# First context's loads pinned among the second projections, and six banks for the first four accumulators

## The chip, the cores and the metric

The kernel runs on one core of a Trainium2 chip. The metric is the time of one execution on the device in microseconds (us). Before the change it is 2506.7 us, the median of three runs (2506.53 to 2509.44).

Engine names as in the profile: PE is TensorE (PEld its weight loads), DVE is VectorE, ACT is ScalarE, POOL is GpSimd, SP is SyncE, which issues nearly all transfers here. Each engine and each queue takes its instructions in order.

## The reference

A decoder layer on x (8 sequences of 100 tokens, width 1024) in three blocks, each followed by "add and layer norm". Cut to what matters here:

```
x1 = layernorm(x + attn(x))              # retention, 8 heads
q, k, v = x1 @ wq, x1 @ wk, x1 @ wv      # "second projections": 16 q heads, 4 k and v heads of 128
q, k = rope(rms_norm(q)), rope(rms_norm(k))
k_ctx, v_ctx = rms_norm(ctx @ wk_ctx), ctx @ wv_ctx     # ctx: 722 rows per sequence
o = softmax(q @ [k_ctx, k].T * scale + causal mask) @ [v_ctx, v]
x2 = layernorm(x1 + o @ wo)
out = layernorm(x2 + (silu(x2 @ w_gate.T) * (x2 @ w_up.T)) @ w_down.T)
```

## The kernel before

Activations lie with their features on the 128 partitions. The 800 tokens are two halves of N = 400 (four sequences each). To keep the precision of float32, every operand is split in a high part (a rounded copy, made by ScalarE, line 67) and a low part (the difference, made by VectorE, line 68), and each product takes three matmuls (`mm3`, lines 86 to 88). A projection of one 128-wide block of outputs for one half (`proj`, lines 100 to 105) is thus 8 x 3 = 24 matmuls into one accumulator bank. PSUM has eight banks, given out by tag: three of "a", four of "s", one of "v" (line 50).

**The place of the change** is the passage from the first block to the second. `out_proj` (lines 217 to 251) computes the output projection of the first attention and the norm after it, half by half. For half 1 the norm is split into parts (`norm_early`, `norm_more`, `norm_late`): seven of the eight blocks of y are centred early (line 298), the last is added at line 240, the correction of the mean comes as a matmul (line 306), those of the variance at lines 300 and 307. Then follow the subtraction of that correction (line 317), the root (`inv_root`, lines 110 to 122: Ln, Exp, Square on ScalarE, lines 113, 116 and 118, and two steps on VectorE, lines 119 and 121), eight multiplications (line 272), eight splits into the tiles z1[1], and eight stores to zd (line 275).

**The second projections** (lines 624 to 655) run over the four key heads kv. Each has six weights w2[kv, i] (i = 0 to 3 queries, 4 keys, 5 values), loaded in groups, for kv = 0 as 0 to 3 and then 4 and 5. Within a group the two halves follow each other, and each half runs over the group's i. One pass of the innermost loop is called a *unit* here; kv = 0 has twelve. A unit is a projection, and then its drain:

- ScalarE squares the accumulator (line 646); GpSimd sums the squares over the partitions (`all_red`, line 126, tile ss).
- `rope` (lines 129 to 139): ScalarE copies the accumulator with its halves swapped into t2 (lines 134 and 135); VectorE multiplies the accumulator by the cosines into t1 (line 136), t2 by the sines (137), and adds the two (138).
- `inv_root` gives the factor r; VectorE multiplies (line 651); the result is split into d, and SP stores it (line 655).
- The unit i = 5 is transposed instead, split and stored (lines 640 to 643).

The accumulator's bank is free once lines 646, 134, 135 and 136 have read it. In this kernel every unit takes its accumulator from the three banks "a"; t2 and r are both PSUM banks with tag "s" (`swapped=` and `at=`).

**The context.** `load_context(b)` brings the context of sequence b: two halves hf of four transfers (tile cs, of the tag "wst" with three buffers, which the weight loads use too), each split into tiles of the tag "big". For sequence 0 it is called ahead of the units i = 4 and 5 of kv = 0 (line 628). Its first reader is `context_keys` in kv = 1 (lines 630 to 634; hf 0 first), the second is in kv = 2.

**The order.** The code is traced in this order, and a planner then sets the order on each engine with simulated times (line 1091), so that instructions move ahead of work written before them. `tc.keep_in_program_order(i)` takes that freedom from i in one direction: i stays behind the instruction that was traced last on the same engine before it. Where the planner finds work for TensorE and where a transfer is issued thus depend on what it believes to be ready.

Of the kernel before, what the change touches and what calls it, by code (L numbers as in the profile page):

```python
# [19 lines left out]
N = NB * T  # L20
KT = D // P
QT = KT // 2
SC, SH = 722, 362
# [16 lines left out]
def decoder_layer(ctx, tc, xT, cT, w1, wo1, w2, wo2, wc, w3, wd, gw, qw, kw, trig, dec, mask, out):  # L40
    nc = tc.nc

    def sbuf(name, bufs, side=None):
        return tc.tile_pool(name=name, bufs=bufs, side=side, reuse_waits="tile")
# [8 lines left out]
    def bank(tag):  # L53
        return ps.tile([P, 512], F32, tag=tag, name=tag, bufs=banks[tag])

    def f32(ap):
        return ap.bitcast(F32)

    def bt(ap):
        return ap.rearrange("p (b t) -> p b t", b=NB)  # L60

    def split(dst, src):

        split2(dst[:, 0], dst[:, 1], src)
# [5 lines left out]
    def load_w(src, w=None, parts=1):  # L70
        st = wp.tile([P, KT * P], F32, tag="wst", name="wst", bufs=3)
        if w is None:
            w = wp.tile([P, 2, KT * P], FR, tag="w", name="w", bufs=4)
        for i in range(parts):
            c = slice(i * KT * P // parts, (i + 1) * KT * P // parts)
            nc.sync.dma_start(out=st[:, c], in_=src[:, c])
            split(w[:, :, c], st[:, c])
        return w
# [11 lines left out]
    def mmw(acc, w, k, rh, rl, start, stop):  # L90
        c = slice(k * P, (k + 1) * P)
        mm3(acc, w[:, 0, c], w[:, 1, c], rh, rl, start, stop)
# [3 lines left out]
    def acc_tag():  # L96
        turn[0] += 1
        return "as"[turn[0] % 2]

    def proj(w, z, n=N, tag="a"):  # L100
        acc = bank(tag)[:, :n]
        for k in range(KT):
            t = z[k // QT]
            mmw(acc, w, k, t[:, 0, k % QT, :n], t[:, 1, k % QT, :n], k == 0, k == KT - 1)
        return acc
# [4 lines left out]
    def inv_root(pool, ss, eps, n=N, pin=False, at=None):  # L110

        r = pool.tile([P, n], F32, tag="r0", name="r0") if at is None else at
        ln = nc.scalar.activation(r, ss, AF.Ln, bias=eps)
        if pin:
            tc.keep_in_program_order(ln)
        nc.scalar.activation(r, r, AF.Exp, scale=-0.5)
        q = pool.tile([P, n], F32, tag="r1", name="r1")
        nc.scalar.activation(q, r, AF.Square)
        nc.vector.scalar_tensor_tensor(q, ss, eps, q, ALU.add, ALU.mult)
        out = q if at is None else at  # L120
        nc.vector.scalar_tensor_tensor(out, q, 3.0, r, ALU.subtract, ALU.mult)
        return out
# [6 lines left out]
    def rope(pool, acc, cosw, sinw, tag="t1", op=ALU.add, swapped=None):  # L129

        t1 = pool.tile([P, N], F32, tag=tag, name=tag)
        t2 = pool.tile([P, N], F32, tag="t2", name="t2") if swapped is None else swapped
        h = P // 2
        nc.scalar.copy(t2[0:h], acc[h:P])
        nc.scalar.copy(t2[h:P], acc[0:h])
        nc.vector.tensor_tensor(bt(t1), bt(acc), cosw[:, None, :].to_broadcast([P, NB, T]), ALU.mult)  # L136
        nc.vector.tensor_tensor(bt(t2), bt(t2), sinw[:, None, :].to_broadcast([P, NB, T]), ALU.mult)
        nc.vector.tensor_tensor(t1, t1, t2, op)
        return t1
# [26 lines left out]
    def big(shape):  # L166
        return bp.tile(shape, FR, tag="big", name="big")
# [9 lines left out]
    def const(v, name):  # L177
        t = cp.tile([P, 1], F32, name=name)
        nc.vector.memset(t, v)
        return t  # L180
# [3 lines left out]
    eps_k = const(128e-6, "eps_k")  # L184
# [238 lines left out]
    with sbuf("l1", 2) as p:  # L423
# [42 lines left out]
        qk, v, oo, ss = {}, {}, {}, {}  # L466
# [104 lines left out]
    with sbuf("ln1", 1) as p:  # L571
        z1 = [out_proj(half, wo1, load_o1, xT, p, 2, p, lambda _: [z1p.tile([P, 2, QT, N], FR, tag="z", name="z")
                                                                 for _ in range(2)], zd) for half in range(2)]
# [3 lines left out]
    ka = kapool.__enter__()  # L577
    cz = []

    def load_context(b):  # L580

        cz.clear()
        for hf in range(2):
            n = SN[hf]
            z = [big([P, 2, QT, SH]) for _ in range(2)]
            for k in range(0, KT, 2):
                cs = wp.tile([P, KT * P], F32, tag="wst", name="cs", bufs=3)
                cs = cs[:, :2 * n].rearrange("p (k n) -> p k n", k=2)
                nc.sync.dma_start(out=cs, in_=cT[b, :, k:k + 2, hf * SH:hf * SH + n])
                split(z[k // QT][:, :, k % QT:k % QT + 2, :n], cs)  # L590
            cz.append(z)

    def context_keys(kv):

        kall = ka.tile([P, 2, SC + T], FR, tag="kall", name="kall")
        wk = load_ws(2 * kv)
        sq = ka.tile([P, SC], F32, tag="ksq", name="ksq", bufs=1)
        ss = ka.tile([P, 6 * P], F32, tag="kss", name="kss", bufs=1)
        row = dr.tile([6, P], F32, tag="row", name="row", bufs=2)
        nc.gpsimd.memset(ss[:, SC:], 1.0)  # L600

        def step(hf):
            n, at = SN[hf], slice(hf * SH, hf * SH + SN[hf])
            acc = proj(wk, cz[hf], n)
            nc.scalar.activation(sq[:, at], acc, AF.Square)  # L605
            nc.gpsimd.partition_all_reduce(ss[:, at], sq[:, at], P, RED.add)  # L606
            nc.scalar.activation(kall[:, 0, at], acc, AF.Copy, scale=kws)
            nc.vector.scalar_tensor_tensor(kall[:, 1, at], acc, kws, f32(kall[:, 0, at]), ALU.mult, ALU.subtract)
            if hf:
                nc.sync.dma_start(out=row.rearrange("c p -> (c p)")[None, :], in_=ss[0:1])  # L610
        return step, (kall, row)
# [9 lines left out]


    early = []
    with sbuf("l2", 2) as p:
        for kv in range(NKV):
            for i0, i1 in ((0, 4), (4, 6)) if kv == 0 else ((0, 2), (2, 4), (4, 6)):
                if (kv, i0) == (0, 4):
                    load_context(0)
                ws = [load_w(w2[kv, i]) for i in range(i0, i1)]
                if (kv, i0) in ((1, 2), (2, 2)):  # L630
                    step, kept = context_keys(kv - 1)
                    early.append(kept)
                if (kv, i0) in ((1, 2), (2, 0), (2, 2), (3, 0)):
                    step(i0 == 0)
                for half in range(2):
                    bs = slice(half * NB, (half + 1) * NB)
                    for i in range(i0, i1):
                        acc = proj(ws[i - i0], z1[half])
                        if i == 5:
                            tr = tokens_first(p, acc).rearrange("p (b d) -> p b d", b=NB)  # L640
                            vs = p.tile([T, NB, 2, P], FR, tag="vs", name="vs", bufs=1)
                            split2(vs[:, :, 0], vs[:, :, 1], tr)
                            nc.sync.dma_start(out=f32(vd[kv, :, bs]), in_=f32(vs))
                            continue
                        sq = p.tile([P, N], F32, tag="sq", name="sq")
                        nc.scalar.activation(sq, acc, AF.Square)
                        ss = all_red(p, sq, "ss")
                        tb = tq if i < 4 else tk
                        t = rope(p, acc, tb[:, 0], tb[:, 1], swapped=bank("s")[:, :N])
                        r = inv_root(p, ss, eps_k, at=bank("s")[:, :N])  # L650
                        nc.vector.scalar_tensor_tensor(
                            t, t, -0.5 if i < 4 else -0.5 * math.sqrt(P), r, ALU.mult, ALU.mult)
                        d = p.tile([P, NB, 2, T], FR, tag="d", name="d", bufs=3)
                        split2(d[:, :, 0], d[:, :, 1], bt(t))
                        nc.sync.dma_start(out=f32(qd[kv, i, :, bs] if i < 4 else kd[kv, :, bs]), in_=f32(d))
# [5 lines left out]
    with sbuf("cx", 2) as p, sbuf("c1", 1) as p1:  # L661
# [6 lines left out]
        for b in range(B):  # L668
            if b > 0:
                load_context(b)  # L670
            for kv in range(NKV):
                if early:
                    kall, row = early.pop(0)
                else:
# [9 lines left out]
                                  in_=f32(qd[kv, :, :, b]).rearrange("h p l t -> p h (l t)"))  # L684
# [21 lines left out]
                s = p1.tile([P, NC, N], F32, tag="s", name="s")  # L706
# [5 lines left out]
                for j, c in enumerate(ORDER):  # L712
                    rows, n, t0 = (R6, N6, T6) if c == 6 else (P, N, 0)
# [35 lines left out]
                for j in (1, 0, 2, 3, 4, 5, 6):  # L749
                    c = ORDER[j]  # L750
                    n = N6 if c == 6 else N
# [4 lines left out]
                r = p.tile([P, N], F32, bufs=1, tag="r0", name="r0")  # L756
# [72 lines left out]
    ws = [[load_w(w3[i, part]) for part in range(2)] for i in range(2)]  # L829
    gs = {}  # L830
    for half in range(2):
        for i in range(2):
            ag, au = (proj(w, z2[half], tag=acc_tag()) for w in ws[i])
            t = temp()
# [163 lines left out]
    with sbuf("ln3", 2, "right") as lnp:  # L998
        ws = []
        for half in range(2):  # L1000
# [3 lines left out]
            for m in range(KT):  # L1004
# [7 lines left out]
                acc = proj(ws[m], z3[half], tag=acc_tag())  # L1012
# [83 lines left out]
```

## Time and profile before

| What | Value |
|---|---|
| median of three runs | 2506.7 us |
| the profiled execution's own time | 2508.7 us |
| its span, first to last instruction | 2506.9 us |
| instructions | 37175 |
| mean granted TensorE clock | 0.995 of full speed |
| all eight cs loads of the first context: casts, subtractions | 64 of each in the whole kernel, 8 between 583.6 and 606.3 us |
| second projections, units of kv = 0 | 575.9 to about 663 us |
| L67 cast of a cs tile, mean | 794 ns on ACT |
| L68 subtraction of a cs tile | 902 to 915 ns on DVE |
| L126 all-reduce of ss, median | 2604 ns on POOL |

The page cuts the span into 40 slices of 63 us, a digit for each: the busy share in tenths (9 is 90% or more).

```profile
PE   8999999997999999999999999999999999999997
DVE  7677877567877688989999999866987777666756
POOL 0111111001445343433434434100000000000000
DMA  7333445774543654554554563675455444389731
```

The tenth slice, 564 to 627 us, holds the passage described above. It is the only one between the first and the last in which TensorE's digit is 7.

### The profile page before, as it was taken

What the parts mean: (1) busy time and instruction counts of PE and PEld (TensorE: products, weight loads), DVE (VectorE), ACT (ScalarE), POOL (GpSimd) and SP (SyncE); (2) the same over time, 40 slices, a digit from 0 to 9 for tenths busy, and PEclk for the clock granted to TensorE, in tenths of its full rate; (3) what the DMA queues carried; (4) which work ended last, traced back from release to release, by engine and by line L of the source; (5) the groups of instructions that cost most, each with busy time, mean ns of one, the idle gap of its engine ahead of it and who ended that gap; (6) DMA issues with size and microseconds to landing.
All of it is one profiled execution on the core that took longest, in us unless ns stands there. A gap on an engine that the chain in (4) does not pass through costs nothing.

```text
span 2506.9 us, 37175 instructions
## 1 busy us (share of the span) xinstructions
PE 2456.2 (98%) x14036; PEld 2435.6 (97%) x14036; DVE 1952.7 (78%) x3110; ACT 1342.0 (54%) x2264; POOL 464.8 (19%) x234
## 2 busy tenths in 40 slices
PE   8999999997999999999999999999999999999997
PEld 8999999997999999999999999999999999999997
DVE  7677877567877688989999999866987777666756
ACT  6667676334767556656566666533544445432221
POOL 0111111001445343433434434100000000000000
PEclk9999999998999999999999999999999999999999
DMA  7333445774543654554554563675455444389731
GB/s 241 111 111 128 134 142 184 241 271 128 170 148 131 215 175 152 166 171 146 165 185 133 174 196 119 208 254 162 136 179 193 168 168 163 120 293 331 261 101 53
DMA packets 224450, 433.96 MB, mean 173 GB/s; under 512 B 47338, under 2 KB 168042, under 8 KB 211854
## 3 DMA queue, kind: packets, MB, share of 16 engines
q1 hardware_dynamic: 223118, 427.39, 51.0%
q0 software_dynamic: 1152, 4.19, 1.1%
q8 instruction: 110, 1.80, 0.3%
q14 instruction: 70, 0.57, 0.1%
HBM read 322.18 MB, written 109.35 MB: 172 GB/s over the span
## 4 chain that ended last, share of the span: by engine, by line
PE 92%; DVE 3%; DMA 2%; ACT 1%; issue 1%; POOL 0%; SPq 0%; DVEq 0%; POOLq 0%
PE a L88 19%; PE a L86 19%; PE a L87 19%; PE s L88 9%; PE s L87 9%; PE s L86 9%; PE v L88 2%; PE v L86 2%; PE v L87 2%; PE s L492 1%; PE s L689 1%; PE s L149 1%; DVE w L68 1%; DMA tp<-in_xT 0%; PE v L484 0%
## 5 line engine op out<-in xcount | busy, mean ns | idle before, releaser
L86 PE MATMUL a<-big,w 128*128 128x400 f32 (+2 forms) x1808 | 610.3, 338 | 10.9 <-ACT big L67 6.8
L87 PE MATMUL a<-big,w 128*128 128x400 f32 (+2 forms) x1808 | 610.2, 338 | 0.0
L88 PE MATMUL a<-big,w 128*128 128x400 f32 (+2 forms) x1808 | 608.5, 337 | 0.0
L67 ACT CAST w<-wst 128x1024 fp32r<-128x1024 f32 (+1 forms) x231 | 239.6, 1039 | 392.9 <-PE a L88 148.7
L68 DVE TENSOR_TENSOR w<-wst,w 128x1024 fp32r<-128x1024 f32 (+1 forms) x231 | 282.7, 1225 | 135.7 <-ACT w L67 134.7
L86 PEld LDWEIGHTS a<-big,w 128*128 128x128 f32 x1808 | 340.5, 188 | 12.9 <-ACT big L67 6.8
L87 PEld LDWEIGHTS a<-big,w 128*128 128x128 f32 x1808 | 341.1, 189 | 1.5 <-DVE big L68 0.6
L88 PEld LDWEIGHTS a<-big,w 128*128 128x128 f32 x1808 | 341.0, 189 | 0.6
L86 PE MATMUL a<-z,w 128*128 128x400 f32 x680 | 235.0, 346 | 21.1 <-DVE t L136 18.6
L88 PE MATMUL a<-z,w 128*128 128x400 f32 x680 | 235.9, 347 | 0.0
L87 PE MATMUL a<-z,w 128*128 128x400 f32 x680 | 235.8, 347 | 0.0
L86 PE MATMUL s<-big,w 128*128 128x400 f32 x664 | 230.5, 347 | 0.1
L88 PE MATMUL s<-big,w 128*128 128x400 f32 x664 | 229.0, 346 | 0.4 <-DVE w L68 0.4
L87 PE MATMUL s<-big,w 128*128 128x400 f32 x664 | 229.1, 345 | 0.0
L126 POOL PARTITION_ALL_REDUCE ss<-sq x56 | 151.2, 2702 | 332.3 <-DMA zd<-y 171.0
L606 POOL PARTITION_ALL_REDUCE kss<-ksq x64 | 166.3, 2599 | 128.6 <-ACT ksq L605 128.1
L86 PEld LDWEIGHTS a<-z,w 128*128 128x128 f32 x680 | 128.3, 189 | 22.9 <-DVE t L136 15.9
L723 ACT ACTIVATE s<-s,rk 128x400 f32<-128x400 f32 x160 | 87.9, 591 | 94.9 <-DVE sm L743 68.6
L88 PEld LDWEIGHTS a<-z,w 128*128 128x128 f32 x680 | 129.0, 190 | 0.3
L87 PEld LDWEIGHTS a<-z,w 128*128 128x128 f32 x680 | 128.3, 189 | 0.2
L86 PEld LDWEIGHTS s<-big,w 128*128 128x128 f32 x664 | 124.6, 188 | 1.4 <-ACT w L67 0.4
L88 PEld LDWEIGHTS s<-big,w 128*128 128x128 f32 x664 | 125.1, 188 | 0.7 <-DVE w L68 0.7
(331 smaller groups left out, 5427.0 us busy)
## 6 DMA issues: line engine op xcount, KB each, us to landing
wst<-in_w SPq DMA_DIRECT2D x135, 512.0 KB
w<-wcd SPq DMA_DIRECT2D x64, 1024.0 KB
wst<-in_wo SPq DMA_DIRECT2D x64, 512.0 KB
hd<-h SPq DMA_DIRECT2D x12, 1400.0 KB
wst<-in_wd SPq DMA_DIRECT2D x64, 256.0 KB
big<-o1d SPq DMA_DIRECT2D x16, 800.0 KB
qd<-d SPq DMA_DIRECT2D x32, 400.0 KB
q<-qd SPq DMA_DIRECT2D x32, 400.0 KB
```

Source lines behind the costliest of these rows:

```text
L67: nc.scalar.copy(hi, src)
L68: nc.vector.tensor_tensor(lo, src, f32(hi), ALU.subtract)
L86: nc.tensor.matmul(acc, lh, rh, start=start, stop=False, skip_group_check=chain)
L87: nc.tensor.matmul(acc, lh, rl, start=False, stop=False, skip_group_check=chain)
L88: nc.tensor.matmul(acc, ll, rh, start=False, stop=stop, skip_group_check=chain)
L126: nc.gpsimd.partition_all_reduce(y, x, P, op)
L149: nc.tensor.transpose(tr[0:T, b * P:(b + 1) * P], vt[:, b * T:(b + 1) * T], ident)
L492: nc.tensor.matmul(bt(o)[:, b], vv[:, b * P:(b + 1) * P], pf[:, b], start=True, stop=True)
L606: nc.gpsimd.partition_all_reduce(ss[:, at], sq[:, at], P, RED.add)
L689: nc.tensor.transpose(tr[0:rows, (c - c0) * P:(c - c0 + 1) * P], vt[:, c * P:c * P + rows], ident)
L723: nc.scalar.activation(sc, sp, AF.Copy, scale=rk[:, c:c + 1])
```

## The change

Three things. `load_context` becomes a generator, `context_steps`, which stops after each transfer and its split; other sequences still run it through at once. For sequence 0 a step is taken ahead of each of eight units of kv = 0 (the four of half 1 in the first group, then the four of i = 4 and 5), and its transfer is kept in program order on SP's queue. The four units of the first group's half 0 (`first`) take their accumulators in turn from the tags "s" and "a" (`acc_tag`), and have t2 and r in SBUF tiles of the pool l2 (the tags "t2" and "r0", which were not used there) in place of two PSUM banks.

```diff
-    def load_context(b):
+    def context_steps(b, pinned=False):
 
         cz.clear()
         for hf in range(2):
...
             for k in range(0, KT, 2):
                 cs = wp.tile([P, KT * P], F32, tag="wst", name="cs", bufs=3)
                 cs = cs[:, :2 * n].rearrange("p (k n) -> p k n", k=2)
-                nc.sync.dma_start(out=cs, in_=cT[b, :, k:k + 2, hf * SH:hf * SH + n])
+                i = nc.sync.dma_start(out=cs, in_=cT[b, :, k:k + 2, hf * SH:hf * SH + n])
+                if pinned:
+                    tc.keep_in_program_order(i)
                 split(z[k // QT][:, :, k % QT:k % QT + 2, :n], cs)
-            cz.append(z)
+                if k == 0:
+                    cz.append(z)
+                yield
+
+    def load_context(b):
+        for _ in context_steps(b):
+            pass
...
     early = []
+    ctx0 = context_steps(0, True)
     with sbuf("l2", 2) as p:
         for kv in range(NKV):
             for i0, i1 in ((0, 4), (4, 6)) if kv == 0 else ((0, 2), (2, 4), (4, 6)):
-                if (kv, i0) == (0, 4):
-                    load_context(0)
                 ws = [load_w(w2[kv, i]) for i in range(i0, i1)]
...
                 for half in range(2):
                     bs = slice(half * NB, (half + 1) * NB)
+
+                    first = (kv, i0, half) == (0, 0, 0)
                     for i in range(i0, i1):
-                        acc = proj(ws[i - i0], z1[half])
+                        if kv == 0 and (half == 1 or i0 == 4):
+                            next(ctx0, None)
+                        acc = proj(ws[i - i0], z1[half], tag=acc_tag() if first else "a")
...
-                        t = rope(p, acc, tb[:, 0], tb[:, 1], swapped=bank("s")[:, :N])
-                        r = inv_root(p, ss, eps_k, at=bank("s")[:, :N])
+                        t = rope(p, acc, tb[:, 0], tb[:, 1], swapped=None if first else bank("s")[:, :N])
+                        r = inv_root(p, ss, eps_k, at=None if first else bank("s")[:, :N])
```

## The prediction

> **What bounds the kernel.** Page first: the engines' busy times. Then the waits of TensorE, which say where its idle time lies; then the stretch in question by windows; then the chain that ended last, in order of time; last the timelines of VectorE and GpSimd.
>
> ```profile
> PE 2456.2 (98%) x14036; PEld 2435.6 (97%) x14036; DVE 1952.7 (78%) x3110; ACT 1342.0 (54%) x2264; POOL 464.8 (19%) x234
> ...
> PE a L86 <- DVE t L136: 18.6, 3, 15.6
> ```
>
> TensorE is busy for 2456.2 of 2506.9 us. Of the 50.7 us of idle time, one wait has 15.6: a matmul into an accumulator bank ("a") that VectorE's L136 must first have read. The windows (columns: length, then busy us of PE, PE's weight load, DVE, ACT, POOL, then the granted clock) put it at the passage from the first norm to the second projections:
>
> ```profile
> 600.00:606.40 6.40, 0.48 (x3) 0.15 (x1) 4.46 (x7) 3.19 (x5) 0.00 (x0) 0.78 0.58 187
> 606.40:615.50 9.10, 0.00 (x0) 0.00 (x0) 9.01 (x19) 5.76 (x12) 2.77 (x1) 0.50 0.74 262
> 615.50:630.00 14.50, 12.53 (x56) 12.19 (x57) 10.94 (x20) 10.26 (x22) 10.32 (x4) 0.82 0.07 28
> 630.00:660.00 30.00, 27.01 (x150) 26.35 (x148) 28.33 (x48) 23.58 (x45) 14.47 (x6) 1.00 0.49 167
> 660.00:690.00 30.00, 29.46 (x166) 29.10 (x165) 23.86 (x40) 20.86 (x41) 14.55 (x6) 1.00 0.53 174
> ```
>
> PE loses 5.92 + 9.10 + 1.97 + 2.99 + 0.54 = 20.5 us between 600 and 690. It also runs 13 matmuls after the long wait at 0.333 us apart (616.10 to 620.6) where they take 0.182 later: 2.0 us. So **22.5 us** is all that this place can give. From 630 to 660 VectorE is busy for 28.33 of 30 us: there, the drain of the units bounds, not TensorE. From 660 on it is not (23.86 of 30).
>
> Why does the drain begin only at 615.5? The chain (start, length, what):
>
> ```profile
> 585.87 0.84 DVE big L68
> 586.72 3.30 DMA cs<-in_cT
> 590.04 0.81 ACT big L67
> 590.88 0.93 DVE big L68
> 591.82 3.18 DMA cs<-in_cT
> 595.02 0.81 ACT big L67
> 595.85 0.91 DVE big L68
> 596.76 1.22 DVE y L317 x3
> ...
> 600.53 0.91 DVE big L68
> 601.46 3.11 DMA cs<-in_cT
> 604.59 0.79 ACT big L67
> ```
>
> These are the eight loads of the first context ("cs") and their splits. They are written after the first eight units, but the planner has put them in the middle of the norm of half 1. Their three buffers go round in a ring (load, cast, subtract, load), and VectorE and ScalarE, whose queues go in order, stand behind them. The norm's Ln is at 603.59, its factor is ready at 607.7, z1[1] is complete at 615.5, and only then does VectorE run the first L136.
>
> **The change, part by part.** Call the twelve units of kv = 0 u0 to u11 in program order; each is 24 matmuls, 4.4 us. From the rows, PE started u3 at 616.1, u4 at 622.6, u5 at 628.5, u8 at 643.0, u9 at 649.5, u10 at 653.9.
>
> *Loads out of the norm.* VectorE loses eight subtractions (7.09 us busy up to 606.4), ScalarE eight casts (6.36 us). What is late next: the last block of the output projection, whose accumulator is added at 590.12 (L240, 0.57). From there the norm's own steps: square 0.54, variance matmul 0.83, L314 0.57, Ln, Exp, Square 0.63 + 0.53 + 0.54, L119 and L121 0.64 + 0.57, eight L272 3.97, eight subtractions of z 3.97; the eight L317 (3.93) fit beside ScalarE's part but for about 0.5. Sum: 590.69 + 13.3 = 604.0 instead of 615.5, 11.5 us earlier. Against that: in the trace the mean's correction (L306) was ready at 590.7 and stood in PE's queue until 594.11. If that 3.4 us stays, the gain is 8. I take 10.2, somewhat above the middle, since the planner times that matmul by VectorE's work, which shrinks. Ends: 8 and 11.5.
>
> *Six banks.* u0 to u3 take s, a, s, a instead of a only; with the third "a", u4 needs no drained bank either. u3 runs at 600.1 instead of 616.1, and u4 follows at 604.5 if z1[1] is there (its first slices are ready soon after the last L272, and then come every 0.5 us, PE takes one each 0.55). So the 15.6 us hole closes as such. But u5 needs u1's L136, u6 u3's, and from u7 on the pairing is the old one (u8 after u5, u9 after u6). Shift the old L136 times (u1 620.6, u3 630.4, u4 635.5, u5 642.3, u6 648.8) by 10.2: u5 starts at 611 (2 us of idle time), u6 at 621 (about 5), u8 at 633, u9 at 639, u10 at 644. TensorE is ahead, then waits again for VectorE: the unit of matmuls that was brought forward is worth nothing in itself. **What counts is the shift of the drain**, because u9 <- u6 is the last wait that binds.
>
> *The loads in their new place.* Each cs load stands on SP's queue behind the last SP instruction traced before it: the first four behind the store of d of u3 to u6, the fifth behind the weight load of i = 5, the last three behind the stores of u8, u9, u10. Old d subtractions end at 639.7 for u3, 647.9 for u4; less 10.2 and plus 3.2 to land (chain above), cs 0 is split at 633, cs 1 at 641. Ahead of u6's L136 (638.6) lie cs 0 and cs 4: 2 x 0.91 = 1.8 us of VectorE. The rest falls where VectorE has 6 us in 30 free, and u10 had some 2 us to spare (u7's L136 at 651.2 for a start at 653.9). First use of the context is the projection whose square is at 686.0, of its second half later; both have tens of us. SP: the weight loads behind a cs wait for nothing new, as each d store was in that queue before.
>
> *t2 and r0 in SBUF for u0 to u3.* Durations alike: L137 takes 574 ns with PSUM, 569 ns where both tiles were in SBUF. But here a rule speaks against the change. The trace first:
>
> ```profile
> 625.24 2.60 POOL L126 PARTITION_ALL_REDUCE ss<-sq  x1 [0.35 <-ACT sq L646]
> ...
> 625.26 2.15 DVE L68 TENSOR_TENSOR d<-t,d 128x400 fp32r<-128x400 f32 x1
> ...
> 640.14 2.28 DVE L68 TENSOR_TENSOR w<-wst,w 128x1024 fp32r<-128x1024 f32 x1
> ```
>
> The subtraction of d takes 0.57 elsewhere; begun with an all-reduce it took 2.15. The one of w, 1.22 elsewhere, took 2.28. The Trainium skill ("SBUF — State Buffer", Who interferes with whom) says that a VectorE instruction with two SBUF inputs shares a read interface with a GpSimd instruction that reads SBUF, and that the second to start is blocked until the first is finished. With t2 and r in PSUM, L137, L138, L121 and L651 had one SBUF input; now 16 instructions have two. By the rule each of four all-reduces could hold VectorE for its 2.6 us: 10.4. The trace is milder: the one above was held 1.6, and the subtraction of w at 632.34, 1.7 us into an all-reduce begun at 630.66, took its normal 1.22. So at most 1.6 for each reduce, 6.4 in all; new hits only where an instruction falls in its first part. I take one, 1.2 us (1.1 and 1.6 were seen); ends 0 and 6.4.
>
> *Rest.* The generator and cz cost nothing on the chip. The four extra tiles may lie where y lay: at most 2.4 us (a store's landing in the chain), once, before u0's L136, and hidden behind z's subtractions; taken as 0.
>
> **Sum**: -10.2 + 1.8 + 1.2 = **-7.2 us**; the profiled span 2506.9 becomes 2499.7, its own time 2508.7 becomes 2501.5, and from the median 2506.7 it is **2499.5**. A change below 0.2% (5.0 us) can't be told from none here. With all ends favourable: -11.5 - 2.7 (stretched subtractions that miss the reduces) = -14; unfavourable: -8 + 1.8 + 6.4 = 0.
>
> **Rivals.** *R1, no change (0.23):* the drain gives it back. All eight splits end up ahead of u6 or u9 in VectorE's order (7.2 us), or the reduces hold several of the new instructions. 10.2 - 7.2 - 3 = 0: 2506.7. For it: VectorE 28.33 of 30; against: the queue order above.
>
> *R2, slower (0.17):* the planner believes a cs load lands sooner than it does. Its cast then stands at the head of ScalarE's queue, the subtraction at that of VectorE's, and the drains behind both wait. Before, ScalarE waited 5.2 us for these eight loads (0.65 each, 1.7 at most), with the loads issued early; now each is issued late, one at a time, and a full landing is 3.2. It decides from 7.2 + 2 (spare) over 8 = 1.2 us each; at 2.2 it costs 17.6 - 9.2 = +8: 2515. Against: the planner now has other work to put in front.
>
> *R3, much faster (0.12):* the planner, with four accumulators in hand, orders the drains so that VectorE has no holes (it idled 3.46 us before u1's L136), and PE stays fed: some 16 of the 22.5 us: 2490.5.
>
> **Numbers.** Forecast 0.48 at 2499.5 (its own range 2493 to 2504). Faster by over 0.2%: most of it (0.45) and R3, 0.57. Within: the rest of it, R1 without its slow tail: 0.25. Slower: 0.18. Range 2490 to 2510: below lies half of R3, above most of R2.
>
> **What would show it.** Right: no cs rows before 606; z's subtractions ending near 605; u3 at once after u2; PE waits for L136 of 2 to 5 us each around 610 to 640, and no wait over 8; VectorE full until some 650; the clock dips less than 0.50. Wrong: ScalarE waiting for cs between 625 and 665 (R2); all-reduces beside L137, L138, L121 or L651 of 1.5 us and more (R1); or the norm no earlier, because PE's queue holds L306 and L300.

## The result

The changed kernel takes 2538.85 us (median of four runs, 2537.49 to 2539.44), the one before 2506.68 beside it: a ratio of 1.0125, with a 95% interval from 1.0113 to 1.0138. It is 32 us slower; the forecast was 7 us faster. The profiled execution took 2537.49 us, with a span of 2535.7.

From the page of the changed kernel, the busy times and two rows of slices:

```profile
PE 2459.5 (97%) x14036; PEld 2437.7 (96%) x14036; DVE 1961.2 (77%) x3110; ACT 1343.7 (53%) x2264; POOL 465.8 (18%) x234
...
PE   8999999998499999999999999999999999999997
...
PEclk9999999999799999999999999999999999999999
```

Little has become longer as work: TensorE is busy for 3.3 us more, of which the sum below puts 1.8 down to its slower clock after waits; the rest is not accounted for. The new idle time lies in one slice, the eleventh (634 to 697 us), which has gone from 9 to 4, and the passage from the norm that was at 7 is now at 8. The waits of TensorE (us in total, times, longest):

```profile
PE a L86 <- ACT w L67: 35.7, 6, 19.7
PE a L86 <- DVE t L136: 10.7, 2, 10.4
```

The wait for a bank (L136, 18.6 before) has shrunk. A wait for *weights* (ScalarE's cast of w, 1.8 us in all before) has grown to 35.7. The windows of the changed kernel (length, then busy us of PE, PE's weight load, DVE, ACT, POOL, then the granted clock) show when:

```profile
600.00:610.00 10.00, 9.69 (x54) 9.36 (x53) 9.96 (x18) 7.03 (x15) 6.85 (x2) 1.00 0.41 149
610.00:620.00 10.00, 3.79 (x21) 3.46 (x19) 9.79 (x14) 7.70 (x16) 6.66 (x3) 0.84 0.11 41
620.00:630.00 10.00, 5.84 (x25) 5.84 (x26) 10.00 (x15) 6.30 (x13) 5.71 (x2) 0.65 0.21 82
630.00:640.00 10.00, 4.43 (x25) 4.10 (x23) 8.91 (x15) 6.59 (x14) 4.68 (x2) 0.86 0.59 187
640.00:650.00 10.00, 0.00 (x0) 0.00 (x0) 7.34 (x13) 4.67 (x9) 0.89 (x1) 0.50 0.42 116
650.00:660.00 10.00, 5.68 (x22) 5.13 (x23) 4.28 (x4) 3.68 (x4) 0.00 (x0) 0.62 0.57 195
...
680.00:690.00 10.00, 0.51 (x2) 0.50 (x2) 2.54 (x5) 2.71 (x4) 0.00 (x0) 0.50 0.73 226
```

The first row is what the change aims at: TensorE works through 600 to 610, where it stood before. Then come three holes. In the first, VectorE is full (9.79 of 10, 10.00): a drain is late. In the second, VectorE and ScalarE run dry too (from 8.91 and 6.59 down to 4.28 and 3.68), and in the third they do little (2.54 and 2.71): no compute engine is full there. The chain of the changed kernel through these two (start, length, what):

```profile
646.83 0.32 SPq L666
647.24 0.39 SPq L589
647.72 5.26 DMA wst<-in_w
653.00 1.05 ACT w L67
654.07 1.24 DVE w L68
655.35 0.70 PE a L88
...
681.73 0.34 SPq L666
682.12 0.43 SPq L589
682.59 5.78 DMA wst<-in_w
688.40 1.05 ACT w L67
689.48 1.24 DVE w L68
690.75 0.70 PE a L88
```

Twice the same six steps: a store of d (L666), a pinned load of the context (L589), and only then the load of weights, with its landing, cast and subtraction, on which TensorE waits. SyncE's own timeline of the changed kernel shows the queue:

```profile
646.83 0.32 SPq L666 DMA_DIRECT2D qd<-d  x1
647.24 0.39 SPq L589 DMA_DIRECT2D cs<-in_cT  x1
647.72 1.08 SPq L76 DMA_DIRECT2D wst<-in_w  x2
...
682.12 0.43 SPq L589 DMA_DIRECT2D cs<-in_cT  x1
682.59 15.64 SPq L76 DMA_DIRECT2D wst<-in_w  x7
```

The two weights of i = 4 and 5 are issued after cs 3 (the load at 647.24), and seven more weight loads, those of kv = 1 first, in a row after cs 7 (682.12). Before, the context's loads were through by 602, and three weight loads went out right behind them, some 40 us ahead of the first unit with i = 4 (643.05):

```profile
578.39 23.44 SPq L589 DMA_DIRECT2D cs<-in_cT  x8
602.28 4.40 SPq L76 DMA_DIRECT2D wst<-in_w  x3
```

In the changed kernel the loads stand in the order in which the buffers of the tag "wst" were asked for in the code: cs 0 to 3, two weights, cs 4 to 7, further weights. It is the place in the queue that costs, more than an occupied buffer. If the three buffers go round in that order, the first of the two weights takes that of cs 1, whose subtraction ended at 641.39. By this estimate its load could have gone out 6.3 us earlier than 647.72, had it not stood behind cs 3 and the store ahead of cs 3.

The sum: TensorE's waits between 600 and 715 are 46.0 us (0.3 + 10.4 + 19.7 + 0.2 + 1.4 + 13.2 + 0.2 + 0.6) against 20.5 before, 25.5 more. Twenty-four matmuls follow waits at half rate (3.6 us lost) against twelve (1.8). Together 27.3 of the 28.8 us between the two spans (2535.7 and 2506.9).

### The profile page after: what moved, and what is told of

Read it like the earlier page. It is cut to its first block, busy times and chain, and to the rows that moved or that the text cites. A ratio compares the mean times of both kernels' runs of the same rounds, so it can differ in the third digit from the quotient of the medians.

```text
span 2535.7 us, 37151 instructions
## 1 busy us (share of the span) xinstructions
PE 2459.5 (97%) x14036; PEld 2437.7 (96%) x14036; DVE 1961.2 (77%) x3110; ACT 1343.7 (53%) x2264; POOL 465.8 (18%) x234
## 4 chain that ended last, share of the span: by engine, by line
PE 92%; DVE 4%; DMA 2%; ACT 1%; issue 1%; SPq 0%; DVEq 0%; ACTq 0%
PE a L88 19%; PE a L86 19%; PE a L87 19%; PE s L88 9%; PE s L87 9%; PE s L86 9%; PE v L88 2%; PE v L86 2%; PE v L87 2%; PE s L492 1%; PE s L700 1%; DMA wst<-in_w 1%; PE s L149 1%; DMA tp<-in_xT 0%; PE v L484 0%
## 5 line engine op out<-in xcount | busy, mean ns | idle before, releaser
L86 PE MATMUL a<-z,w 128*128 128x400 f32 x664 | 230.8, 348 | 45.8 <-ACT w L67 35.1
L88 PE MATMUL a<-z,w 128*128 128x400 f32 x664 | 231.4, 349 | 0.5 <-DVE w L68 0.5
L87 PE MATMUL a<-z,w 128*128 128x400 f32 x664 | 231.3, 348 | 0.0
L86 PEld LDWEIGHTS a<-z,w 128*128 128x128 f32 x664 | 126.3, 190 | 47.7 <-ACT w L67 36.4
L88 PEld LDWEIGHTS a<-z,w 128*128 128x128 f32 x664 | 126.9, 191 | 1.6 <-DVE w L68 1.5
L87 PEld LDWEIGHTS a<-z,w 128*128 128x128 f32 x664 | 126.2, 190 | 0.0
```

Of the source, the lines that this page charges most:

```text
L86: nc.tensor.matmul(acc, lh, rh, start=start, stop=False, skip_group_check=chain)
L87: nc.tensor.matmul(acc, lh, rl, start=False, stop=False, skip_group_check=chain)
L88: nc.tensor.matmul(acc, ll, rh, start=False, stop=stop, skip_group_check=chain)
```

## The experiments

Theories: **RING**, the loads into the buffers of "wst" go out in traced order, so that a weight traced after a pinned cs is issued after it; **PIN**, SP is held by the pins whatever the buffers; **PORT**, t2 and r in SBUF hold VectorE beside the all-reduces. The kernel before, run beside each group, had a median of 2506.7 to 2507.2.

| Run | us, median | ratio to before, 95% interval |
|---|---|---|
| e1_own_ring | 2508.1 | 1.0002 (0.9993 to 1.0011) |
| e2_not_pinned | 2505.7 | 0.9996 (0.9988 to 1.0005) |
| e3_pinned_no_banks | 2535.5 | 1.0112 (1.0097 to 1.0127) |
| e4_banks_only | 2506.4 | 0.9999 (0.9991 to 1.0008) |
| e5_own_ring_no_banks | 2504.9 | 0.9989 (0.9983 to 0.9996) |
| e6_own_ring_psum | 2507.3 | 1.0001 (0.9993 to 1.0009) |
| e7_own_ring_r_psum | 2506.0 | 0.9995 (0.9987 to 1.0003) |
| e8_weights_ahead | 2520.6 | 1.0052 (1.0036 to 1.0067) |
| e9_ring_first_pin | 2513.1 | 1.0029 (1.0018 to 1.0040) |
| e10_own_first_pin | 2506.7 | 1.0001 (0.9993 to 1.0010) |
| e11_own_r_psum_first_pin | 2507.8 | 1.0004 (0.9996 to 1.0013) |
| e12_splits_off_vectore | 2505.4 | 0.9992 (0.9983 to 1.0000) |

**Which half of the change costs.** Four runs, each with one thing taken out. A ring of its own for the pinned loads:

```diff
-cs = wp.tile([P, KT * P], F32, tag="wst", name="cs", bufs=3)
+cs = pinned.tile([P, 2 * SH], F32, tag="cs", name="cs", bufs=1)   # pinned: the pool l2
```

> Only change against the changed kernel: the pinned cs loads have a tile tag of their own (one buffer), and no longer take their place among the weights in the ring of three 'wst' buffers. Theory RING (the weight loads of i = 4 and 5 and of kv = 1 take their buffers behind the pinned cs loads, so they are issued late and TensorE waits 19.7 + 13.2 us for weights, and starts cold twice): both waits go, 2538.9 falls by some 35 to about 2504 (2498 to 2510). Theory PORT (t2 and r in SBUF hold VectorE beside the all-reduces, and that is the loss): stays above 2525. Theory PIN (SP stands behind stores of d, whatever the buffers): stays above 2525.

The pins taken out (`context_steps(0)` in place of `context_steps(0, True)`):

> Only change: the eight steps stay where they are, but their transfers are not kept in program order. RING: the planner moves cs and weights ahead again, no wait for weights over 5 us, about 2503 (2496 to 2510); the cs splits are back in the norm and its end is late again. PORT: still above 2525.

The six banks taken out (`first = False`):

> Only change: the first four units take 'a' banks and have t2 and r in PSUM, as before; the loads stay pinned in the shared ring. RING: both waits for weights stay, 2533 to 2545. PORT: falls to 2510 or less, since the stretched VectorE instructions (9 us) go.

Only the six banks kept (`load_context(0)` at its old place, no steps):

> Only the six banks: load_context at its old place and unpinned, the first four units with six banks and t2, r in SBUF. RING: no wait for weights; about 2503 (2497 to 2510), the hole at 600 us partly filled, 9 us of VectorE stretched by the all-reduces giving most of that back. PORT: above 2520.

The loss stays with pins *and* the shared ring (e3, 2535.5), and goes with either of them removed (e1 and e2). Own ring, the same pins: 30.8 us less. So PIN falls, since e1 has every pin, and PORT as the main cause falls with e3, which is only 3.4 us under the changed kernel. (In e2 the planner puts six of the eight splits back ahead of z's subtractions. These still end 7.7 us earlier than before, at 607.9, and the time is that of the kernel before.) The waits of TensorE in e1_own_ring:

```profile
PE a L86 <- ACT d L67: 13.5, 1, 13.5
PE a L86 <- ACT big L67: 6.9, 1, 6.9
PE a L86 <- DMA w<-wcd: 5.3, 2, 4.7
PE a L86 <- ACT w L67: 2.9, 4, 1.1
```

The waits for weights are down to 1.1 at most, and none of them lies between 600 and 715. The 13.5 us hole ahead of u6 is left, and e1 ends where the kernel before is: it trades one hole for another. A ring of its own does two things, though: it changes the order, and it leaves the weights three buffers to themselves. The next runs keep the shared ring.

**One wait at a time.** The weights of i = 4 and 5 traced ahead of the steps, in the ring as it is:

```diff
+if (kv, i0, half) == (0, 0, 1):
+    ahead = [load_w(w2[0, i]) for i in (4, 5)]     # and ws = ahead at (0, 4)
```

> Against the changed kernel only this: the loads of weights i = 4 and 5 are written ahead of the pinned cs loads, so that they have their buffers of the shared ring first; cs still shares the ring, and the weights of kv = 1 stay behind. RING: of the two waits for weights the first (19.7 us) goes, the second (13.2) stays: about 2518 (2512 to 2526). If pinning itself held the weights back, both stay: above 2530.

And only the first step pinned, so that cs 1 to 7 don't each wait for a store:

```diff
-if pinned:
+if pinned and (hf, k) == (0, 0):
```

> Against the changed kernel only this: of the eight steps the first alone is kept in program order; cs still shares the ring of three buffers with the weights. RING: the weights of i = 4 and 5 still take their buffers behind cs 0 to 3, but these no longer wait for one store each, so the weights come some 10 to 15 us earlier: both waits together 5 to 15 us in place of 32.9, 2510 to 2522. If the ring alone counted and not the pins: above 2530; if the pins alone counted: 2506 or less.

In e8_weights_ahead the first wait is gone and the second is there at 11.8 us; in e9_ring_first_pin one wait of 11.7 us is left of the two. (Both show the bank's hole ahead of u6 as well.) From the waits of e8:

```profile
PE a L86 <- ACT w L67: 14.7, 5, 11.8
PE a L86 <- ACT d L67: 12.8, 1, 12.8
```

Both times lie where RING put them: each group of weights is as late as the context's loads traced ahead of it. e8 has the same buffers and pins as the changed kernel and only another order of requests, and the wait of the weights that were moved is gone. Why the planner issues them in this order stays open; that the order of the requests decides is shown only by these edits.

**What is the plan worth without that loss?** Own ring (two buffers) in all of these. First the loads alone, with `first = False`:

> The loads alone, freed of the shared ring: cs pinned one per unit with a tag of its own (two buffers), the first four units with 'a' banks and t2, r in PSUM as before. Theory SHIFT (the prediction's: the norm ends 9.5 us earlier, the drain starts as much earlier, and this is what the time follows): 2498 to 2502. Theory FULL (VectorE has no room for the cs splits and the all-reduces' holds at the new place): 2505 to 2509.

Then the six banks, with t2 and r of u0 to u3 in PSUM, and with r alone in PSUM:

> As the run with its own ring, but t2 and r of the first four units in PSUM again; their accumulators still take s, a, s, a (cs with two buffers). Theory PORT2 (the 13.5 us hole ahead of u6 comes from VectorE instructions with two SBUF inputs held by the all-reduces, 1.1 to 1.5 us each): the hole falls below 6 us and the time to about 2498 (2493 to 2502). Theory ORDER (the hole comes from u6 needing the bank of u3, whose drain is behind those of u0 to u2): the hole stays over 9 us, 2504 or more.

> As the run with its own ring, but only r of the first four units in PSUM again, t2 still in SBUF (cs with two buffers). PORT2: L121 and L662 are held no longer, L137 still is (1.6 us): between the two, about 2502. ORDER: 2504 or more.

The loads alone (e5) have the lowest median of all kernels here, 2.4 us (0.11%) under the one before: less than SHIFT asked for, and at the edge of FULL. With t2 and r in PSUM (e6), the longest bank wait falls to 5.7 us, as PORT2 had it, yet the time doesn't follow: four waits for a bank add up to 11.4 us, 2.3 are for z1[1], and the matmuls at half rate lose 5.4 (1.8 before). e7 has the shortest sum of waits in this stretch (15.0 us, 18.8 in e5), and lies between, not to be told from the kernel before. Two us in these traces don't carry over to the medians: the profiled execution of e5 was the slowest of its 21 (2507.4), that of e7 one of its fastest (2504.9).

In the changed kernel the norm ends 9.5 us earlier. What becomes of that when the loads alone are moved? The matmuls that followed a wait in e5_own_ring_no_banks:

```profile
610.47 0.70 PE L86 MATMUL a<-z,w 128*128 128x400 f32 x1 [10.95 <-DVE t L136]
622.54 0.42 PE L86 MATMUL a<-z,w 128*128 128x400 f32 x1 [1.52 <-ACT d L67]
637.07 0.42 PE L86 MATMUL a<-z,w 128*128 128x400 f32 x1 [1.17 <-DVE t L136]
644.32 0.42 PE L86 MATMUL a<-z,w 128*128 128x400 f32 x1 [2.64 <-ACT d L67]
680.14 0.40 PE L86 MATMUL a<-big,w 128*128 128x362 f32 x1 [2.54 <-DMA w<-wcd]
```

The same matmuls stood at 616.10, 628.52, 643.05, 649.48 and 681.74 before: 5.6, 6.0, 6.0, 5.2 and then 1.6 us ahead. Without the six banks the norm itself comes only 5.6 us earlier (z's subtractions from 605.96, in the changed kernel from 602.01, before from 611.59). The fourth matmul of the fence is u9's first; it waits 2.64 us (1.82 before), and TensorE then runs at half rate for some 3 us. The last one waits 2.5 us for the context's own weight, whose load stands behind cs 7 on SP (0.5 before). Of the 4.4 us by which the lead shrinks from 6.0 to 1.6, the longer wait is 0.8, the half rate 1.4 and the wait for the weight 2.0. Two runs tried to win the last part back (theory TAIL), with the first step alone pinned:

> As the run with its own ring and no banks, but only the first step pinned, so that the load of the context's own weight (w from wcd) is not behind the last pinned cs. Theory TAIL (of the 6 us won at u3 to u8, 2 are given back by that wait and 1.6 by the clock): the wait for wcd falls from 2.5 to under 1 us, 2501 to 2504. Else: as that run, 2505.

> As the run with its own ring and r in PSUM (t2 in SBUF, six banks), but only the first step pinned. If six banks add anything to moving the loads: 2500 to 2503, below the run without banks; if the time follows the drain alone: the same as it within 2 us.

They don't decide it. The load of wcd, freed from cs 7, now stood behind a store of d and went out no earlier: at 675.48 in e10 and 674.27 in e11, against 673.25 in e5. The same matmul waited 4.5 and 3.1 us in place of 2.5; the profile puts these waits down to ScalarE's L113 and VectorE's L121, neither of which reads or writes its accumulator, so what it waited for is not shown. The profiled execution of e10 was also its slowest, 5.1 us over the median. Last, the subtractions off VectorE; this run leaves out the low part of the first context:

```diff
-split(z[k // QT][:, :, k % QT:k % QT + 2, :n], cs)
+nc.scalar.copy(dst[:, 0], cs)
+nc.scalar.activation(dst[:, 1], cs, AF.Copy, scale=0.0)
```

> As the run with its own ring and no banks (2504.9, 2.4 us under before), but the low parts of the first context are not computed: ScalarE writes zeros in place of VectorE's eight subtractions (8 x 0.91 = 7.3 us; ScalarE gets as many more). Theory FULL (the 9.5 us won at the norm's end are eaten because VectorE must do the splits among the drains): 3 to 6 us faster still, 2499 to 2502. Theory QUEUE (what is lost is waits of ScalarE for late cs transfers and of TensorE for the context's own weight): no change within 2 us, 2503 to 2507.

VectorE's 27.2 busy us between 640 and 680 (35.9 in e5) are no help: 2505.4. So FULL falls in the form in which it was stated: VectorE's eight subtractions at their new place don't set the time. (ScalarE took over their work, 33.2 busy us for 28.9, so its own room is not tested.) QUEUE fits, with 2.3 us of waiting for wcd and 4.4 us lost by matmuls at half rate (2.7 in e5) in its trace. No run removed all these waits at once, so what would be left of the lead without them stays open.

**PORT, by itself.** VectorE and GpSimd in the changed kernel; a VectorE instruction of 400 columns takes 0.57 us when nothing holds it:

```profile
617.15 1.86 DVE L121 SCALAR_TENSOR_TENSOR r<-r,r 128x400 f32<-128x400 f32 x1
...
621.42 2.11 DVE L121 SCALAR_TENSOR_TENSOR r<-r,r 128x400 f32<-128x400 f32 x1
...
625.93 2.11 DVE L121 SCALAR_TENSOR_TENSOR r<-r,r 128x400 f32<-128x400 f32 x1
...
616.85 2.60 POOL L126 PARTITION_ALL_REDUCE ss<-sq  x1 [1.41 <-DVE r L119]
621.11 2.86 POOL L126 PARTITION_ALL_REDUCE ss<-sq  x1 [1.66 <-DVE r L119]
625.62 2.86 POOL L126 PARTITION_ALL_REDUCE ss<-sq  x1 [1.66 <-DVE r L119]
```

Each of these three L121, now with both inputs in SBUF, begins 0.3 us into an all-reduce and is held. In this kernel that comes from the order: the all-reduce waits for L119 (which frees its ss), and L121 is what comes next on VectorE but for one PSUM instruction. In e1 VectorE's order is another one: a single L121 is held, and two subtractions of d, which had two SBUF inputs before the change too. In all, seven instructions were held for 9.2 us between 600 and 680 in the changed kernel; four, 4.2 us, in the kernel before; one, 1.2 us, in e3 without the six banks; in e1 and e7, which differ in where r lies and in cs's buffers, 11.9 and 3.7. What these holds cost in time was not measured by themselves.

## Why the prediction was wrong

**The step that failed** is the one that priced SP at nothing: "SP: the weight loads behind a cs wait for nothing new, as each d store was in that queue before." The stores were in the queue, but the next weights had stood *ahead* of them (issued from 602.28 on, the first store of d at 627.44). The step asked what each transfer waits for, and not where it stands in the queue. cs and weights take their buffers from one ring, so the weights traced after a pinned cs go out behind it. Measured: 19.7 + 13.2 us of waiting for weights where 0 was put; with a ring of its own (e1), none in this stretch.

A second step failed, and its number hid it: the 10.2 us that were put down to moving the loads. z's subtractions (start, length of all eight) in the kernel before, with the six banks alone (e4), with the loads alone (e5), and in the changed kernel:

```profile
611.59 3.97 DVE L68 TENSOR_TENSOR z<-y,z 128x400 fp32r<-128x400 f32 x8
607.79 3.97 DVE L68 TENSOR_TENSOR z<-y,z 128x400 fp32r<-128x400 f32 x8
605.96 3.97 DVE L68 TENSOR_TENSOR z<-y,z 128x400 fp32r<-128x400 f32 x8
602.01 3.97 DVE L68 TENSOR_TENSOR z<-y,z 128x400 fp32r<-128x400 f32 x8
```

They end at 605.98 in the changed kernel, where 605.3 was forecast. That is luck: the loads give 5.6 us, and 3.8 come from the six banks, with which the last block of y is added earlier (L240 at 585.36, before at 590.12). From the end of L240 to that of z's subtractions were 13.3 us in the forecast and are 20.1 in the changed kernel. PE's L306 still comes 3.2 us after L240, and the eight L317 (3.94), which were to fit beside ScalarE's part, run on VectorE ahead of L314.

The rest of the prediction, part by part:

- *What bounds, and why the drain begins late*: the cs splits did hold the norm up, by 5.6 us.
- *Six banks*: right in kind. u3 and u4 follow without a hole, u5 waits 0.3 us (2 was said), u6 10.4 (5 was said). That the banks by themselves bring nothing is shown by e4 (0.9999).
- *Port*: the mechanism right, the term too small. One hit of 1.2 us was taken, 6.4 the end; six of the sixteen instructions were held, 7.9 us, and with one more 9.2 in all (1.2 in e3, 4.2 before). The hits were counted as chance; three of the six come from the order, as VectorE's own L119 starts the all-reduce.
- *Loads in their new place*: two splits were put ahead of u6's L136, 1.8 us. In the changed kernel none is (L136 at 636.56, the first split's subtraction at 637.04), in e5 one. e12 shows that it hardly matters.
- *The shift sets the time*: not shown by any run. Freed from the ring, the loads win 2.4 us (e5) and not 7.2: 5.6 us at the norm's end, and most of that given back by the wait for wcd and by the clock. Nor does the time follow the norm's end from run to run: it comes 9.2 us earlier than before in e1, 7.7 in e2, 5.6 in e5 and 3.8 in e4, for 2508.1, 2505.7, 2504.9 and 2506.4 us.
- *R2* had the sign, and ScalarE did wait more for cs (16.0 us for the eight loads in place of 5.2, so 2.0 each), but TensorE's new waits were for weights, not for drains behind those casts.

## What to carry over

In this kernel, pinning a load held back more than that load: what stood behind it in the queue, and with it the loads that were traced later and took their buffers from the same ring. Before a load is pinned late, list what else draws on its buffers, and give it buffers of its own if the others are loaded ahead of their use. When a number comes out as forecast, take the parts of the change one at a time before counting its reason as right. And where a tile moves from PSUM to SBUF, look at what its reader stands next to in time, not at its duration alone.

## Not expected of the hardware

- TensorE dropped to half rate (0.33 us from one matmul to the next for some 3 us, in place of 0.18) after a wait of only 2.64 us in e5, at 644.3, and after 1.82 us at the same place in e12. Before, a wait of 1.82 us at 649.5 had no such effect, nor had one of 2.54 us at 680.1 in e5: the length of the wait alone doesn't decide. The Trainium skill ("TensorE: Matmul & The Clock Gate", Part 1) speaks of an idle window of about 3.4 us that runs freely; in these runs less idle time was enough.
- An all-reduce of 2.6 us doesn't hold a VectorE instruction with two SBUF inputs to its end: the L121 begun at 617.15 ended at 619.01, 0.44 us before the reduce did, so that it was let in some 1.6 us after the reduce's start; for those begun at 621.42 and 625.93 it was 1.85 us. The spans of GpSimd are rough in the profile, so these figures are too.
